# Issuing the next load ahead of the exchange of the slot that has landed

## The chip, the core and the metric

The kernel runs on one core of a Trainium2 chip. The core has a matrix engine (TensorE, PE in the profile; its weight loads are shown as PEld), a vector engine (VectorE, DVE), a scalar engine (ScalarE, ACT), a general engine (GpSimd, POOL) and an engine that here only waits and issues transfers (SyncE, SP). Sixteen DMA engines move data between the device's memory and the on-chip memory; ScalarE and SyncE each have a queue of transfers of their own, which both feed the same sixteen. The metric is the device time of one execution in microseconds; less is better.

## What is computed

```python
def reference(x, itok_B_0_7, L0_cond_weights):      # x: (128, 128, 1024) float32
    w = weights[subjects]                            # (8, 128, 128) -> (128, 128, 128)
    out = jnp.einsum('bct,bcd->bdt', x, w)
    return x + out
```

Each of 128 samples, a matrix of 128 channels by 1024 times, is multiplied by one of eight 128 x 128 weight matrices, which its index picks, and added to itself. The sum with x is had by adding the identity to the weights. Read are 64 MiB of x and 0.5 MiB of weights, written are 64 MiB.

## The kernel before

The 128 samples are handled four at a time: 32 turns (NT), each with a slot of 2 MiB of x_all, of which there are 12 (SLOTS). A slot is loaded, exchanged, multiplied, overwritten with the result and stored from the same place. A slot has two halves h (H = 2) of two samples each (G = 2).

**Load.** `load` (line 142) issues two transfers of 1 MiB on ScalarE's queue, one for each half. A transfer puts two successive channel rows of a sample on one partition, so that it moves long pieces. The two samples of a half then lie one on the lower and one on the upper 64 partitions, each with its even channels in the first 1024 columns and its odd ones in the second.

**Exchange.** `trade` (line 154) mends that on ScalarE, by six copies of 64 partitions x 1024 (line 152): for each half the upper partitions' first columns go to `spare` (tensor aside), then the lower partitions' second columns go to their place, then `spare` goes to the lower partitions' second columns. After that one sample fills all partitions, its even channels on the lower ones and its odd ones on the upper ones; weights and identity are sorted the same way at the start. The semaphore s_moved counts the copies done. At the end of the exchange s_ready is raised by two, one for each half.

**Multiply and copy.** `multiply` (line 202) waits for the weights of a half (s_go) and for s_ready, and multiplies into PSUM; `copy` (line 217, VectorE) writes the result of a half back over the slot and raises s_added; `place` (line 195, VectorE) adds weights and identity for what comes next.

**Store.** SyncE waits for s_added and issues the stores in order (lines 300 to 308): one slot each for the first 20 turns, two slots each for the last 12. The very last is issued at line 329. The first store is written from pieces of 4 KB, the others from pieces of 16 or 32 KB. GpSimd waits for each store to land and raises s_empty for the slot that became free (lines 296 to 298). s_empty starts with 7 free slots.

**What sets the order on ScalarE.** Four slots are loaded at once (AHEAD = 4, line 267). Then the loop at line 272 runs 28 times over: wait until slot i has landed (s_in), exchange it, wait for a free slot (s_empty), issue the load of slot i + 4. The last four slots are exchanged behind the loop (line 277). Each engine works through its own instructions strictly in this order, so what stands behind a wait waits too.

Of the kernel before, what the change touches and what calls it, by code (L numbers as in the profile page):

```python
# [30 lines left out]
G = 2  # L31
H = 2
# [3 lines left out]
SLOTS = 12  # L36
# [14 lines left out]
R = 2  # L51

AHEAD = 4
# [5 lines left out]
def transfer(nc, engine, out, in_):  # L59

    later, nc._always_lower_symbolic_ap = nc._always_lower_symbolic_ap, False
    ins, outs = engine.lower_ap_dma(in_), engine.lower_ap_dma(out)
    nc._always_lower_symbolic_ap = later
    return engine.add_instruction(
        mybir.InstDMACopy(
            name=nc.get_next_instruction_name(),
            engine=engine.engine,
            ins=ins,  # L70
            outs=outs,
            mode="Copy",
            cce_op=ALU.bypass,
            queue=QUEUES[engine.engine],
        )
    )
# [3 lines left out]
def kernel(  # L80
# [7 lines left out]
    nc = tc.nc  # L88
    B, C, T = x.shape
# [3 lines left out]
    def sbuf(name, *shape, dtype=F32):  # L93
        return ctx.enter_context(nc.sbuf_tensor(name, list(shape), dtype)).ap()
# [5 lines left out]
    x_all = sbuf("x_all", C, SLOTS * H * G * T)  # L100
# [6 lines left out]
    A = C // R  # L107
    eye = sbuf("eye", C, 1, D)
    mark = sbuf("mark", 1, 1)
    aside = sbuf("aside", C, T)  # L110
    spare = [aside[h * A : (h + 1) * A] for h in range(H)]
# [17 lines left out]
    s_ready = tc.alloc_semaphore("s_ready")  # L129
# [4 lines left out]
    s_eye = tc.alloc_semaphore("s_eye")  # L134
    s_moved = tc.alloc_semaphore("s_moved")
# [3 lines left out]
    def emptied(i):  # L139
        return DMA * (i // SLOTS)  # L140

    def load(k, slot, first):
        for h in range(H):
            transfer(
                nc,
                nc.scalar,
                x_all[:, bass.ds(slot * (H * G * T) + h * G * T, G * T)],
                x[bass.ds(first + h * G, G)].rearrange("h (b r) t -> (h b) (r t)", r=ROWS),
            ).then_inc(s_in[k], DMA)

    def move(out, in_):
        return nc.scalar.copy(out, in_)  # L152

    def trade(k, slot):
        nc.scalar.wait_ge(s_in[k], DMA * H).then_inc(s_in[k], -DMA * H)  # L155
        sides = [
            (
                x_all[A:, bass.ds(slot * (H * G * T) + h * G * T, T)],
                x_all[:A, bass.ds(slot * (H * G * T) + (h * G * T + T), T)],
            )  # L160
            for h in range(H)
        ]
        for h in range(H):
            move(spare[h], sides[h][0]).then_inc(s_moved, 1)
        for h in range(H):
            nc.scalar.wait_ge(s_moved, 1).then_inc(s_moved, -1)
            move(sides[h][0], sides[h][1]).then_inc(s_moved, 1)
        for h in range(H):
            nc.scalar.wait_ge(s_moved, 1).then_inc(s_moved, -1)
            move(sides[h][1], spare[h]).then_inc(s_moved, 1)  # L170
        nc.scalar.wait_ge(s_moved, H).then_inc(s_moved, -H)
        nc.scalar.wait_ge(s_eye, R).then_inc(s_ready, H)

    def store(i, n):
        at = i % SLOTS * H * G * T
# [25 lines left out]

    def multiply(slot, h):
        nc.tensor.wait_ge(s_go, 1).then_inc(s_go, -1)
        nc.tensor.wait_ge(s_ready, 1).then_inc(s_ready, -1)  # L204
        for q in range(h * G, (h + 1) * G):
            for t in range(0, T, N):
                at = slot * (H * G * T) + (q * T + t)
                mm = nc.tensor.matmul(  # L208
                    ps[h][:, q % G, t : t + N],
                    ws[q][:, 0, :],  # L210
                    x_all[:, bass.ds(at, N)],
                    start=True,
                    stop=True,
                )
        mm.then_inc(s_product, 1)
# [6 lines left out]
    with tc.tile_critical():  # L222

        nc.sync.dma_start(
            w_raw, weights.rearrange("s (u j) d -> (s u) (j d)", j=S)
        ).then_inc(s_wall, DMA)
        nc.sync.dma_start(given, subjects.rearrange("(o b) -> o b", o=1)).then_inc(s_given, DMA)

        nc.vector.memset(zeros, 0.0).then_inc(s_zeros, 1)  # L229
        nc.tensor.wait_ge(s_zeros, 1)  # L230
        for _ in range(IDLE):
            nc.tensor.matmul(  # L232
                ps[P_SLOTS - 1][:, G - 1, :N], zeros[:, :D], zeros, start=True, stop=True
            )

        nc.vector.wait_ge(s_wall, DMA)
        for r in range(R):  # L240
            nc.vector.transpose(  # L241
                w_mid.rearrange("p (e r h w j) -> p r j h e w", e=4, r=R, h=4, w=8)[:, r],
                w_raw.rearrange("p (j r d) -> p r j d", r=R, d=D)[:, r],
            ).then_inc(s_sort, 1)
        nc.vector.memset(index[:, B:], 0).then_inc(s_index, 1)
        nc.vector.wait_ge(s_given, DMA)
        nc.vector.tensor_scalar(near, given, -S, S - 1, ALU.max, ALU.min).then_inc(s_index, 1)  # L247
        nc.vector.wait_ge(s_index, 2)
        nc.vector.tensor_scalar(wrap, near, 0, S, ALU.is_lt, ALU.mult).then_inc(s_index, 1)  # L249
        nc.vector.wait_ge(s_index, 3)  # L250
        nc.vector.tensor_tensor(index[:, :B], near, wrap, ALU.add).then_inc(s_index, 1)  # L251

        nc.gpsimd.wait_ge(s_zeros, 1)
        for r in range(R):
            if r:
                nc.gpsimd.wait_ge(s_eye, r)
            nc.gpsimd.affine_select(  # L257
                eye[:, 0],
                eye[:, 0] if r else zeros[:, :D],
                [[-1, D]],  # L260
                ALU.not_equal,
                1.0,
                base=r - r * R * A,
                channel_multiplier=R,
            ).then_inc(s_eye, 1)

        for i in range(AHEAD):
            load(i % AHEAD, i, i * (H * G))
        nc.scalar.wait_ge(s_eye, R)
        nc.scalar.copy(mark, eye[:1, 0, :1])  # L270
        nc.gpsimd.wait_ge(s_eye, R).then_inc(s_empty, SLOTS - 1 - AHEAD)
        with nc.scalar.Fori(0, NT // AHEAD - 1) as turn:
            for k in range(AHEAD):
                trade(k, (turn * AHEAD + k) % SLOTS)
                nc.scalar.wait_ge(s_empty, 1).then_inc(s_empty, -1)
                load(k, (turn * AHEAD + (k + AHEAD)) % SLOTS, turn * (AHEAD * H * G) + (k + AHEAD) * H * G)
        for i in range(NT - AHEAD, NT):
            trade(i % AHEAD, i % SLOTS)

        nc.vector.wait_ge(s_sort, R)  # L280
        nc.vector.transpose(w_late, w_mid).then_inc(s_sort, 1)  # L281

        def sort(engine, o, v):
            engine.tensor_copy(  # L284
                w_all[32 * v : 32 * (v + 1), 2 * o : 2 * (o + 1), :],
                w_late[32 * o : 32 * (o + 1)].rearrange(
                    "c (e u r d) -> c u r e d", e=2, u=2, r=R
                )[:, v % 2, v // 2],
            ).then_inc(s_sort, 1)

        nc.vector.wait_ge(s_sort, R + 1)
        nc.gpsimd.wait_ge(s_sort, R + 1)
        for o in range(4):
            for v in range(4):
                sort(nc.gpsimd if v == 3 else nc.vector, o, v)
        nc.gpsimd.wait_ge(s_added, 1).then_inc(s_empty, 1)
        for i in range(SLOTS, NT):
            nc.gpsimd.wait_ge(s_slot[i % SLOTS], emptied(i)).then_inc(s_empty, 1)

        for i in [*range(NT - SLOTS), *range(NT - SLOTS, NT, PAIR)]:  # L300
            n = 1 if i < NT - SLOTS else PAIR
            nc.sync.wait_ge(s_added, (i + n) * H)
            if i == 0:
                nc.sync.dma_start(
                    out[: H * G].rearrange("g d t -> d g t"), xs[0]
                ).then_inc(s_slot[0], DMA)
            elif i + n < NT:
                store(i, n).then_inc(s_slot[i % SLOTS], DMA)


        nc.vector.wait_ge(s_index, 4)
        nc.vector.wait_ge(s_sort, SORTED)
        nc.vector.wait_ge(s_eye, R)
        subject = subjects_of(slice(0, H * G))
        for h in range(H):
            place(h, subject)
        with nc.vector.Fori(0, NT) as turn:  # L317
            subject = subjects_of(turn + 1)
            for h in range(H):
                copy(turn % SLOTS, h)  # L320
                place(h, subject)
        with nc.tensor.Fori(0, NT) as turn:
            for h in range(H):
                multiply(turn % SLOTS, h)
# [39 lines left out]
```

## Time and profile before

| | |
|---|---|
| time, median of 3 runs | 324.16 us (324.02 to 324.26) |
| the profiled execution's own time | 324.05 us |
| its span, first to last instruction | 322.1 us |
| PE busy | 247.5 us (77%) |
| ACT busy | 198.7 us (62%) |
| DVE busy | 181.5 us (56%) |
| PEld busy | 102.2 us (32%) |
| moved by the DMA engines | 134.76 MB, mean 418 GB/s |

Busy times of engines are read as shares of the span; the issue of a transfer isn't counted as busy. For the DMA engines, the share is the mean over all sixteen. A row of the timeline gives the start, the duration, the engine, the line and the operation, with the idle time ahead of it and what ended it in brackets. Rows of ACTq and SPq are issues of transfers on ScalarE's and SyncE's queues.

### The profile page before, as it was taken

How to read it: one execution, taken by the hardware profiler on the slowest of the kernel's cores; microseconds unless marked ns; L12 is line 12 of the kernel's file. 1: busy time of each engine (PE TensorE's matmuls, PEld its weight loads, DVE VectorE, ACT ScalarE, POOL GpSimd, SP SyncE). 2: the span in 40 equal slices, each digit the busy share in tenths (PEclk: the TensorE clock that was granted, in tenths of full speed). 3: DMA queues.
4: the chain of work that ended last, by engine and by line, in shares of the span. 5: the costliest groups of instructions: out<-in, count | busy, mean ns of one | idle time of the engine just before them, and what ended most of it. 6: DMA issues, size and time to landing. Idle time of an engine off the chain costs nothing. (4 is left out here: it accounts for less than half of the span.)

```text
span 322.1 us, 3002 instructions
## 1 busy us (share of the span) xinstructions
PE 247.5 (77%) x528; PEld 102.2 (32%) x528; DVE 181.5 (56%) x217; ACT 198.7 (62%) x194; POOL 2.5 (1%) x10
## 2 busy tenths in 40 slices
PE   7499988888888888888888599598884989992000
PEld 3144333333333333333333144233332434440000
DVE  4717766666666666666666617447552666775000
ACT  1777777777777777777775772757727699900000
POOL 0200000000000000000000000000000000000000
PEclk9879999999999999999999969789997999999555
DMA  8999999999999999999999999999999999999994
GB/s 326 395 452 392 407 433 433 403 429 429 435 427 427 448 423 439 413 419 423 427 437 433 442 407 423 431 431 433 446 415 411 427 454 407 429 439 431 419 431 203
DMA packets 7731, 134.76 MB, mean 418 GB/s; under 512 B 1457, under 2 KB 1458, under 8 KB 2098
## 3 DMA queue, kind: packets, MB, share of 16 engines
q1 hardware_dynamic: 4658, 67.64, 49.7%
q10 hardware_dynamic: 3072, 67.11, 49.0%
q14 instruction: 1, 0.01, 0.0%
HBM read 67.63 MB, written 67.11 MB: 418 GB/s over the span
## 5 line engine op out<-in xcount | busy, mean ns | idle before, releaser
L208 PE MATMUL ps<-x_all,w 128*128 x512 | 237.7, 619 | 42.7 <-PEq L204 42.3
L220 DVE COPY x_all<-ps 128x2048 f32 x64 | 146.7, 2292 | 107.5 <-DVEq L219 107.5
L208 PEld LDWEIGHTS ps<-x_all,w 128*128 128x128 f32 x512 | 98.2, 197 | 182.2 <-issue 182.0
L152 ACT COPY aside<-x_all 64x1024 f32 (+1 forms) x64 | 66.7, 1042 | 75.2 <-ACTq L155 74.4
L152 ACT COPY x_all<-aside 64x1024 f32 (+1 forms) x64 | 66.8, 1044 | 1.6
L152 ACT COPY x_all<-x_all (+1 forms) x64 | 63.7, 1040 | 0.8
L197 DVE TENSOR_TENSOR w<-w_all,eye 128x128 f32<-128x128 f32 x132 | 31.9, 283 | 0.8 <-issue 0.8
L232 PE MATMUL ps<-x_all 128*128 128x512 f32 x16 | 9.8, 782 | 1.7 <-DVE x_all L229 1.7
L232 PEld LDWEIGHTS ps<-x_all 128*128 128x128 f32 x16 | 4.0, 255 | 6.7 <-issue 5.0
L270 ACT ACT_TABLE_LOAD x1 | 1.3, 1283 | 6.2 <-issue 6.2
L284 DVE COPY w_all<-x_all 32x256 f32<-32x256 f32 x12 | 3.9, 327 | 0.4
L241 DVE STREAM_TRANSPOSE x_all<-x_all 128x512 f32<-128x512 f32 x2 | 2.0, 1076 | 2.9 <-DMA x_all<-in_L_cond_weights_dram 2.9
L284 POOL COPY w_all<-x_all 32x256 f32<-32x256 f32 x4 | 1.7, 426 | 6.6 <-DVE x_all L281 6.5
L281 DVE STREAM_TRANSPOSE x_all<-x_all 128x1024 f32<-128x1024 f32 x1 | 1.2, 1225 | 0.0
L229 DVE MEMSET x_all<- 128x512 f32 x1 | 0.5, 485 | 1.0 <-SPq L222 1.0
L247 DVE TENSOR_SCALAR x_all<-x_all 1x128 int32<-1x128 int32 x1 | 0.2, 215 | 0.6 <-DMA x_all<-in_itok_B_dram 0.6
L257 POOL TENSOR_SCALAR_AFFINE_SELECT eye<-x_all 128x128 f32<-128x128 f32 x1 | 0.3, 295 | 1.4 <-DVE x_all L229 1.4
L251 DVE CUSTOM_DVE_ANT_0 index<-x_all 1x256 uint16<-1x256 uint16 x1 | 0.3, 280 | 0.0
L257 POOL TENSOR_SCALAR_AFFINE_SELECT eye<-eye 128x128 f32<-128x128 f32 x1 | 0.3, 294 | 0.1
L249 DVE TENSOR_SCALAR x_all<-x_all 1x128 int32<-1x128 int32 x1 | 0.2, 214 | 0.0
L270 ACT COPY mark<-eye 1x1 f32<-1x1 f32 x1 | 0.2, 190 | 0.0
L351 POOL MEMSET const-bfloat16-1.0<- 128x1 bf16 x1 | 0.1, 102 | 0.0
(5 smaller groups left out, 0.4 us busy)
## 6 DMA issues: line engine op xcount, KB each, us to landing
x_all<-in_x_dram ACTq DMA_DIRECT2D x64, 1024.0 KB, 10.2
out_dram<-x_all SPq DMA_DIRECT2D x20, 2048.0 KB, 53.1
out_dram<-x_all SPq DMA_DIRECT2D x6, 4096.0 KB, 42.6
x_all<-in_L_cond_weights_dram SPq DMA_DIRECT2D x1, 512.0 KB, 3.5
x_all<-in_itok_B_dram SPq DMA_DIRECT2D x1, 0.5 KB
```

Of the source, the lines that this page charges most:

```text
L152: return nc.scalar.copy(out, in_)
L197: copy = nc.vector.tensor_tensor(ws[q], w_all[:, bass.ds(subject[q], 1), :], eye, ALU.add)
L208: mm = nc.tensor.matmul(ps[h][:, q % G, t : t + N], ws[q][:, 0, :], x_all[:, bass.ds(at, N)], start=True, stop=True,)
L220: nc.vector.tensor_copy(mine, ps[h].rearrange("d g t -> d (g t)")).then_inc(s_added, 1)
L229: nc.vector.memset(zeros, 0.0).then_inc(s_zeros, 1)
L232: nc.tensor.matmul(ps[P_SLOTS - 1][:, G - 1, :N], zeros[:, :D], zeros, start=True, stop=True)
L241: nc.vector.transpose(w_mid.rearrange("p (e r h w j) -> p r j h e w", e=4, r=R, h=4, w=8)[:, r], w_raw.rearrange("p (j r d) -> p r j d", r ...
L251: nc.vector.tensor_tensor(index[:, :B], near, wrap, ALU.add).then_inc(s_index, 1)
L257: nc.gpsimd.affine_select(eye[:, 0], eye[:, 0] if r else zeros[:, :D], [[-1, D]], ALU.not_equal, 1.0, base=r - r * R * A, channel_multipli ...
L270: nc.scalar.copy(mark, eye[:1, 0, :1])
L281: nc.vector.transpose(w_late, w_mid).then_inc(s_sort, 1)
L284: engine.tensor_copy(w_all[32 * v : 32 * (v + 1), 2 * o : 2 * (o + 1), :], w_late[32 * o : 32 * (o + 1)].rearrange("c (e u r d) -> c u r e ...
```

## The change

The function `trade` is split. `landed(k)` waits for slot i; the wait for a free slot and the load of slot i + 4 come next, and the exchange stands behind them. In the exchange, the two copies of the middle step become one over both halves (64 x 2 x 1024), behind a wait for both copies into `spare`; the two copies back wait for it. s_ready is raised by one for a slot, and TensorE waits for it only at the first half. The exchange doesn't wait for s_eye any more. The copy into `mark` raises s_moved by two, so that the first wait at the head of the loop is met.

```diff
-    def trade(k, slot):
+    def landed(k):
         nc.scalar.wait_ge(s_in[k], DMA * H).then_inc(s_in[k], -DMA * H)
-        sides = [
-            (
-                x_all[A:, bass.ds(slot * (H * G * T) + h * G * T, T)],
-                x_all[:A, bass.ds(slot * (H * G * T) + (h * G * T + T), T)],
-            )
-            for h in range(H)
-        ]
+
+    def trade(slot):
+        base = slot * (H * G * T)
+        both = x_all[:, bass.ds(base, H * G * T)].rearrange("c (h s t) -> c s h t", h=H, s=G)
         for h in range(H):
-            move(spare[h], sides[h][0]).then_inc(s_moved, 1)
-        for h in range(H):
-            nc.scalar.wait_ge(s_moved, 1).then_inc(s_moved, -1)
-            move(sides[h][0], sides[h][1]).then_inc(s_moved, 1)
+            move(spare[h], both[A:, 0, h]).then_inc(s_moved, 1)
+        nc.scalar.wait_ge(s_moved, 2 * H).then_inc(s_moved, -2 * H)
+        move(both[A:, 0], both[:A, 1]).then_inc(s_moved, 1)
+        nc.scalar.wait_ge(s_moved, 1).then_inc(s_moved, -1)
         for h in range(H):
-            nc.scalar.wait_ge(s_moved, 1).then_inc(s_moved, -1)
-            move(sides[h][1], spare[h]).then_inc(s_moved, 1)
-        nc.scalar.wait_ge(s_moved, H).then_inc(s_moved, -H)
-        nc.scalar.wait_ge(s_eye, R).then_inc(s_ready, H)
+            move(both[:A, 1, h], spare[h]).then_inc(s_moved, 1)
+        nc.scalar.wait_ge(s_moved, H).then_inc(s_ready, 1)
...
         nc.tensor.wait_ge(s_go, 1).then_inc(s_go, -1)
-        nc.tensor.wait_ge(s_ready, 1).then_inc(s_ready, -1)
+        if h == 0:
+            nc.tensor.wait_ge(s_ready, 1).then_inc(s_ready, -1)
...
-        nc.scalar.copy(mark, eye[:1, 0, :1])
+        nc.scalar.copy(mark, eye[:1, 0, :1]).then_inc(s_moved, H)
...
             for k in range(AHEAD):
-                trade(k, (turn * AHEAD + k) % SLOTS)
+                landed(k)
                 nc.scalar.wait_ge(s_empty, 1).then_inc(s_empty, -1)
-                load(k, (turn * AHEAD + (k + AHEAD)) % SLOTS, turn * (AHEAD * H * G) + (k + AHEAD) * H * G)
+                load(
+                    k,
+                    (turn * AHEAD + (k + AHEAD)) % SLOTS,
+                    turn * (AHEAD * H * G) + (k + AHEAD) * H * G,
+                )
+                trade((turn * AHEAD + k) % SLOTS)
         for i in range(NT - AHEAD, NT):
-            trade(i % AHEAD, i % SLOTS)
+            landed(i % AHEAD)
+            trade(i % SLOTS)
```

On ScalarE, one turn of the loop (that of slot 0 and of the load of slot 4) stands in this order before; ISA rows set registers or wait, and the names in brackets are the semaphores waited for:

```order
L152 ISA [waits s_in0]
L152 COPY aside<-x_all 64x1024
L152 ISA
L152 COPY aside<-x_all 64x1024
L152 ISA [waits s_moved]
L152 COPY x_all<-x_all 64x1024
L152 ISA [waits s_moved]
L152 COPY x_all<-x_all 64x1024
L152 COPY x_all<-aside 64x1024 [waits s_moved] x2
L64 ISA [waits s_moved,s_eye,s_empty]
L64 ISA
L66 DMA x_all<-in_x_dram 128x2048
```

The same turn of the changed kernel, from its wait for slot 0 to the last copy back:

```order
L64 ISA [waits s_in0,s_empty]
L64 ISA
L66 DMA x_all<-in_x_dram 128x2048
L64 ISA
L66 DMA x_all<-in_x_dram 128x2048
L152 ISA
L152 COPY aside<-x_all 64x1024
L152 ISA
L152 COPY aside<-x_all 64x1024
L152 ISA [waits s_moved]
L152 COPY x_all<-x_all 64x2x1024
L152 COPY x_all<-aside 64x1024 [waits s_moved]
```

The load and the wait for a free slot have moved from behind the copies to ahead of them, and one double copy stands where two single ones stood.

At the end of ScalarE's loop, before, the wait for the last free slot and the last load close the loop, and the exchange of slot 28 follows:

```order
L152 COPY x_all<-aside 64x1024 [waits s_moved] x2
L64 ISA [waits s_moved,s_eye,s_empty]
L64 ISA
L66 DMA x_all<-in_x_dram 128x2048
L64 ISA
L66 DMA x_all<-in_x_dram 128x2048
L272 REGISTER_ALU
L272 COMPARE_AND_BRANCH
L152 COPY aside<-x_all 64x1024 [waits s_in0]
```

In the changed kernel the exchange of slot 27 stands between the last load and the loop's end:

```order
L66 DMA x_all<-in_x_dram 128x2048
L152 ISA
L152 COPY aside<-x_all 64x1024
L152 ISA
L152 COPY aside<-x_all 64x1024
L152 ISA [waits s_moved]
L152 COPY x_all<-x_all 64x2x1024
L152 COPY x_all<-aside 64x1024 [waits s_moved]
L152 ISA
L152 COPY x_all<-aside 64x1024
L268 REGISTER_ALU [waits s_moved]
L268 COMPARE_AND_BRANCH
```

Five exchanges now stand behind the last load where four stood. The transfers, their sizes and their number are the same.

## The prediction

> **What bounds the kernel now.** First the transfers over the whole span, since the kernel reads and writes 64 MiB each and computes little per byte. The page's slices (each a fortieth of the span, the tenths being the busy share of the 16 DMA engines) and its queue rows (packets, MB, share of the 16 engines' time):
>
> ```profile
> DMA  8999999999999999999999999999999999999994
> DMA packets 7731, 134.76 MB, mean 418 GB/s; under 512 B 1457, under 2 KB 1458, under 8 KB 2098
> q1 hardware_dynamic: 4658, 67.64, 49.7%
> q10 hardware_dynamic: 3072, 67.11, 49.0%
> ```
>
> Every slice but the first and the last is at 9, and the stores (q1) and loads (q10) together took 98.7% of what 16 engines had to give in 322.1 us. Next the same by stage, in the view of windows (window, its length, busy time of PE, PEld, DVE, ACT, POOL, then TensorE's granted clock, the DMA share and GB/s):
>
> ```profile
> 0.00:4.00 4.00, 2.33 (x3) 1.18 (x4) 0.51 (x2) 0.00 (x0) 0.79 (x6) 1.00 0.57 172
> 4.00:28.00 24.00, 18.91 (x35) 7.59 (x34) 13.43 (x27) 15.34 (x16) 1.71 (x4) 0.86 1.00 430
> 28.00:44.00 16.00, 14.58 (x34) 6.10 (x33) 11.42 (x15) 11.47 (x12) 0.00 (x0) 1.00 1.00 394
> 44.00:172.00 128.00, 110.27 (x249) 45.88 (x248) 82.66 (x91) 96.11 (x95) 0.00 (x0) 1.00 1.00 429
> 172.00:256.00 84.00, 66.86 (x134) 27.30 (x133) 44.84 (x52) 51.10 (x50) 0.00 (x0) 0.90 1.01 430
> 256.00:268.00 12.00, 10.81 (x26) 4.51 (x25) 7.89 (x10) 11.04 (x11) 0.00 (x0) 1.00 0.98 418
> 268.00:292.00 24.00, 23.73 (x54) 9.62 (x52) 18.06 (x21) 13.61 (x14) 0.00 (x0) 1.00 1.02 432
> 292.00:316.00 24.00, 0.00 (x0) 0.00 (x0) 2.69 (x3) 0.00 (x0) 0.00 (x0) 0.61 1.00 429
> 316.00:322.00 6.00, 0.00 (x0) 0.00 (x0) 0.00 (x0) 0.00 (x0) 0.00 (x0) 0.50 0.31 131
> ```
>
> From 4 to 316 us the DMA share is 1.00, and the rate stays near 430 GB/s whether loads run alone (4 to 28), both directions (44 to 256) or stores alone (292 to 316). Only 28 to 44 is poorer, at 394. Last, what waits at the end: the chain's last piece, SyncE's last issue and its last wait.
>
> ```profile
> 294.34 0.48 DVE w L197 x2
> 295.12 0.56 SPq L66 DMA_DIRECT2D out_dram<-x_all  x1
> SPq L360 <- DMA out_dram<-x_all: 25.4, 1, 25.4
> ```
>
> All computing is over at 294.8, and then 25.4 us go to stores that were queued. So **the DMA engines bound the whole kernel**. A load that starts earlier only goes ahead of a store on the same engines. The sum: 0.57 x 4 + 24 + 16 + 128 + 84.8 + 11.8 + 24.5 + 24 + 0.31 x 6 = 317 us of work for 16 engines, and some 5 us of start and end that the change doesn't touch. No byte, no packet size and no store is changed.
>
> **The change part by part.** One slot's turn on ScalarE, from the timeline (start, duration, in brackets the idle time ahead), and the costs of single copies:
>
> ```profile
> 58.28 1.15 ACTq L66 DMA_DIRECT2D x_all<-in_x_dram  x2
> 59.79 2.11 ACT L152 COPY aside<-x_all 64x1024 f32 x2 [2.01 <-ACTq L155]
> 61.92 1.99 ACT L152 COPY x_all<-x_all  x2
> 63.94 2.11 ACT L152 COPY x_all<-aside 64x1024 f32 x2
> 66.55 1.15 ACTq L66 DMA_DIRECT2D x_all<-in_x_dram  x2
> 7.48 0.19 ACT L270 COPY mark<-eye 1x1 f32<-1x1 f32 x1
> 263.05 2.11 ACT L152 COPY aside<-x_all 64x1024 f32<-64x1024 f32 x2 [0.30 <-ACTq L155]
> L152 ACT COPY x_all<-x_all (+1 forms) x64 | 63.7, 1040 | 0.8
> ```
>
> A turn takes 66.55 - 58.28 = 8.27 us: 1.15 for the two DMA issues, 0.36 to the first copy, 6.26 of exchange (59.79 to 66.05) and 0.50 to the next issue. ScalarE never waits for data here: it is itself the pace of the loads, one 2.1 MB slot in 8.27 us, 254 GB/s of the 429, and the stores get the rest.
>
> *The middle copies become one.* A copy of one element took 0.19 us and one of 1024 per partition 1.04, so 0.85 is per 1024 elements; 0.19 + 2 x 0.85 = 1.89 us in place of 1.99. That saves 0.10.
>
> *Fewer waits, but each for the copy just ahead.* Before, the copies go in two independent strands (h = 0 and 1), so that a copy waits for the one two places back, and the gaps between pairs are 0.02 us. After, the double copy waits for both copies ahead, and the copies back wait for the double copy. The nearest row of such a wait is the 0.30 us ahead of the exchange at 263.05, where the next exchange waits for the last copy of the one before. Two of these: +0.60, less the two gaps of 0.02. The exchange becomes 2.11 + 0.30 + 1.89 + 0.30 + 2.11 = 6.71 us, **0.45 longer, not shorter**. Bounds: 6.11 with no bubble at all (0.15 shorter); 7.30 if the double copy costs two whole ones (2.08) and each bubble is like the 0.50 ahead of an issue (1.04 longer). I take 6.71, as the 0.30 row is the same kind of wait. A turn then takes 8.72 us and loads flow at 240 GB/s; stores take what is left. In the sum for the end it is nothing while the store queue has work, and it does: stores land 53 us after their issue.
>
> ```profile
> out_dram<-x_all SPq DMA_DIRECT2D x20, 2048.0 KB, 53.1
> ```
>
> The wait on s_eye that goes had been met before the copy into mark at 7.48, which waits for it too, and TensorE's second wait on s_ready was met by the same signal as its first. Both are at nothing; a gain is excluded because neither was ever the last thing waited for.
>
> *The load ahead of the exchange.* The first two issues move from 16.53 to about 10, when slot 0 has landed; the first exchange starts some 1.5 us later and ends 2 later, and so does the first store.
>
> ```profile
> 9.76 2.11 ACT L152 COPY aside<-x_all 64x1024 f32 x2 [2.09 <-ACTq L155]
> 16.53 1.16 ACTq L66 DMA_DIRECT2D x_all<-in_x_dram  x2
> ```
>
> The load queue wasn't dry at 16.53 (DMA share 1.00 from 4 to 28), so this fills no hole: **0 us**. Its bounds are what the poor stretch from 28 to 44 can give or take, 1.3 us either way (B and C below).
>
> *The wait for a free slot now stands ahead of the exchange.* From 172 us on the loads are held by s_empty. What is queued behind that wait on ScalarE is now the exchange of a slot that has long landed, and behind it TensorE, VectorE and SyncE. While eight older slots are waiting to be stored, nobody on the DMA side sees it. At the end it counts. The rows there (ScalarE; TensorE with 16 matmuls a slot; VectorE's last copy):
>
> ```profile
> 255.06 1.16 ACTq L66 DMA_DIRECT2D x_all<-in_x_dram  x2
> 256.48 2.11 ACT L152 COPY aside<-x_all 64x1024 f32<-64x1024 f32 x2 [2.79 <-ACTq L155]
> 263.21 28.68 PE L208 MATMUL ps<-x_all,w 128*128 x64 [1.19 <-PEq L204]
> 206.09 17.17 PE L208 MATMUL ps<-x_all,w 128*128 x32 [3.39 <-PEq L204]
> 224.84 7.13 PE L208 MATMUL ps<-x_all,w 128*128 x16 [1.58 <-PEq L204]
> ```
>
> The last load goes out at 255.06 when store 19 has landed, which the DMA rate sets and the change leaves. Before, slot 27 was exchanged by then and four remained. After, five remain: 27 starts at 256.48 and is ready at 263.2, TensorE starts it at 263.7 and needs 28.68 / 4 = 7.17 us a slot for five, more than ScalarE's 6.71 + 0.30, so till 299.6; VectorE ends 2.9 later (294.8 against 263.21 + 28.68 = 291.9), and the last store is issued at 302.8 in place of 295.1. The DMA engines come to it when? It and what follows is two slots, 4.19 MB, 9.8 us at 429. Stores end at about 316 + 0.31 x 6 = 317.9, so its turn is at 308.1. With about 1 us from issue to first packet (the first packets begin by 4 - 0.57 x 4 = 1.7 us, the first issue stands at 0.91), **4 us of slack are left of 12**. If the wait lets TensorE's clock fall, 17.17 - 2 x 7.13 = 2.9 us more go, and 1 is left.
>
> By the Trainium skill, "TensorE: Matmul & The Clock Gate", Part 1, about 3.4 us of idleness bring the clock to half. The trace agrees (17.17 us after a gap of 3.39, none of it after 1.58). By that rule the wait moved ahead of the exchange costs TensorE its clock, as reckoned above; without it the last store would be in time by 4 us rather than 1.
>
> **Sum**: 0 at the start, 0 in the middle, 0 at the end, under the cover of the store queue. The profiled execution took 324.05 us, against a median of 324.16: the changed kernel takes 324.1.
>
> **The rivals.**
> *A: the tail is uncovered (slower).* If the exchange costs its upper bound, ScalarE rather than TensorE paces the five last slots: 256.48 + 5 x (7.30 + 0.30) = 294.5, then 0.5 + 7.2 + 2.9 make 305.1, with 2.9 for the clock 308.0, and the last store is issued at 308.3 and has packets at 309.3, 1.2 us late. A free-slot signal later by another us adds as much; together 326.3. It decides once the last store is issued after 307. For it: the margin is the smallest in the kernel, and both steps that eat it are this change's. Against: it needs both upper bounds.
> *B: the dip at 28 to 44 us heals (faster).* It is worth (430 - 394) x 16 us / 430 = 1.3 us, hence 322.7. There store 0, written from 4 KB pieces (the page counts 2098 - 1458 = 640 packets between 2 and 8 KB), meets the loads. The changed kernel has a longer load queue there and store 0 comes 2 us later, so the mixture is another. For: it is the only poor stretch. Against: the same pieces and the same loads are still to be moved.
> *C: the dip gets deeper,* since more loads are queued when store 0's small pieces come: doubled, +1.3 us, 325.4.
> *D: the DMA rate as such rises.* In the trace the best long stretch, 432, lies 0.6% above the 429 of the middle, so at most 128 + 84 us x 0.006 = 1.3 us, again 322.8; nothing in the change alters packets, so I count it with B.
> The Trainium skill's "DMA: Bandwidth & Descriptors", Where 436 GB/s comes from, gives 435 GB/s as the ceiling of the 16 engines; by it an estimate of the least transfer time is 134.76 MB / 435 = 310 us, 7 below the 317 used, but no stretch here holds it.
> That the change doesn't do what it says, as the loads after 172 us are held by free slots and not by the exchange, gives the forecast's time as well.
>
> **How the numbers follow.** A measurement of this kernel tells about 0.2% (0.65 us) from no change. Forecast 0.72 (within 0.2%), A 0.10, C 0.08, B and D 0.10. So faster 0.10, same 0.72, slower 0.18. The range takes in the forecast, most of B (322.9) and C and nearly all of A (326.0); about 0.1 is left out.
>
> **What would show it.** Right: DMA share 1.00 from 4 to 316 us again; the first pair of loads issued near 10 us; an exchange of about 6.7 us with two gaps of 0.3; turns of 8.7 us up to about 170 us; last store issued near 303 to 306, and SyncE's last wait down from 25.4 to some 15 us. Wrong: a window after 292 us with a DMA share under 0.95 (A), or a rate between 28 and 44 us that isn't 394 (B, C). What would overturn the whole: a time below 322, as it would need bytes moved faster than in any stretch of this trace.

## The result, and the profile after

| | time, median | range | ratio to the kernel before |
|---|---|---|---|
| before, beside it | 324.11 us (13 runs) | 323.88 to 324.34 | |
| changed | 323.59 us (13 runs) | 323.14 to 323.92 | 0.9983 (0.9975 to 0.9992) |

The kernel is 0.17% faster, 0.5 us, which lies within the 0.2% of the forecast and in its range. The profiled execution took 323.66 us, with a span of 321.7.

The DMA queues of the changed kernel (packets, MB, share of 16 engines) and its slices:

```profile
DMA  8999999999999999999999999999999999999994
q1 hardware_dynamic: 4658, 67.64, 49.7%
q10 hardware_dynamic: 3072, 67.11, 48.9%
```

The same packets, and 98.6% of what 16 engines had. The windows of the changed kernel (TensorE's clock, DMA share and GB/s are the last three columns):

```profile
4.00:28.00 24.00, 17.43 (x32) 6.99 (x31) 12.11 (x27) 13.62 (x13) 1.71 (x4) 0.86 1.00 427
28.00:44.00 16.00, 14.26 (x33) 5.91 (x32) 11.81 (x13) 12.13 (x10) 0.00 (x0) 1.00 1.06 437
44.00:172.00 128.00, 107.48 (x239) 44.50 (x237) 79.77 (x91) 87.76 (x73) 0.00 (x0) 0.99 1.00 426
172.00:256.00 84.00, 64.09 (x130) 26.32 (x131) 44.95 (x51) 51.82 (x43) 0.00 (x0) 0.92 1.00 428
268.00:292.00 24.00, 23.80 (x55) 9.81 (x53) 18.44 (x21) 20.13 (x17) 0.00 (x0) 1.00 1.01 430
292.00:316.00 24.00, 7.45 (x17) 2.95 (x16) 8.07 (x9) 0.00 (x0) 0.00 (x0) 0.77 1.01 429
```

The DMA share stays at 1.00 up to 316 us. What moved is inside: TensorE and VectorE now work into the window from 292 on (7.45 and 8.07 us, where before there were 0 and 2.69). The poor stretch from 28 to 44 has gone from 394 to 437 GB/s; but the window behind it, first of the kernel before and then of the changed one, shows where it went:

```profile
44.00:60.00 16.00, 13.46 (x31) 5.54 (x30) 10.67 (x12) 11.85 (x13) 0.00 (x0) 1.00 1.02 435
```

```profile
44.00:60.00 16.00, 13.35 (x31) 5.43 (x29) 9.25 (x13) 11.62 (x10) 0.00 (x0) 1.00 0.95 400
```

From 28 to 60 us together that is (394 + 435) / 2 = 414.5 before and 418.5 after: 4 GB/s over 32 us, 0.3 us of transfer time. A piece counts in the window in which it begins, so a share can exceed 1.00 (1.06 beside the 437), and single windows swing by some per cent.

ScalarE's first turn in the timeline of the changed kernel, and the tail: ScalarE's last load with the exchange of slot 27 behind it, TensorE's last five slots, SyncE's last two issues (a merged row, from the first's start to the second's end) and its last wait:

```profile
10.22 1.16 ACTq L66 DMA_DIRECT2D x_all<-in_x_dram  x2
11.55 2.11 ACT L152 COPY aside<-x_all 64x1024 f32 x2 [3.86 <-issue]
13.85 1.90 ACT L152 COPY x_all<-x_all  x1 [0.19 <-ACTq L162]
15.86 2.11 ACT L152 COPY x_all<-aside 64x1024 f32 x2
18.45 1.15 ACTq L66 DMA_DIRECT2D x_all<-in_x_dram  x2
```

```profile
255.44 1.16 ACTq L66 DMA_DIRECT2D x_all<-in_x_dram  x2
256.77 2.11 ACT L152 COPY aside<-x_all 64x1024 f32 x2 [1.83 <-issue]
```

```profile
263.61 35.90 PE L204 MATMUL ps<-x_all,w 128*128 x80 [1.12 <-PEq L200]
```

```profile
287.70 15.59 SPq L66 DMA_DIRECT2D out_dram<-x_all  x2
```

```profile
SPq L362 <- DMA out_dram<-x_all: 17.4, 1, 17.4
```

The first loads go out at 10.22 in place of 16.53. At the end TensorE does five slots in one go behind the last load, till 299.5, and the last store's issue ends at 303.3, 7.6 us later than before (295.12 + 0.56 = 295.7); SyncE waits 17.4 us for it in place of 25.4. Those 7.6 us came out of the cover, the time in which stores that are already queued keep the DMA engines busy, and not out of the time of the kernel.

### The profile page after: what moved, and what is told of

The parts are those of the page before. It is cut to its first block, busy times and chain, and to the rows that moved or that the text cites. A ratio compares the mean times of both kernels' runs of the same rounds, so it can differ in the third digit from the quotient of the medians.

```text
span 321.7 us, 2843 instructions
## 1 busy us (share of the span) xinstructions
PE 247.7 (77%) x528; PEld 102.2 (32%) x528; DVE 181.4 (56%) x217; ACT 195.7 (61%) x162; POOL 2.5 (1%) x10
## 5 line engine op out<-in xcount | busy, mean ns | idle before, releaser
L152 ACT COPY x_all<-x_all (+1 forms) x32 | 60.7, 1897 | 6.2 <-ACTq L162 5.7
```

## The experiments

The kernels that end in "again" are the same as their namesakes, run side by side on another chip.

| run | time | ratio to the kernel before (interval) |
|---|---|---|
| e1, before, store 0 from 16 KB | 323.90 us | 0.9991 (0.9980 to 1.0002) |
| e2, changed, store 0 from 16 KB | 323.63 us | 0.9983 (0.9974 to 0.9991) |
| e3, reorder alone | 324.20 us | 1.0000 (0.9991 to 1.0009) |
| e11, reorder alone, again | 324.24 us | 0.9997 (0.9988 to 1.0006) |
| e4, double copy alone | 324.01 us | 0.9991 (0.9980 to 1.0002) |
| e12, double copy alone, again | 323.65 us | 0.9974 (0.9964 to 0.9984) |
| e10, the changed kernel again | 323.98 us | 0.9992 (0.9982 to 1.0002) |
| e7, no exchange | 323.23 us | 0.9960 (0.9945 to 0.9975) |
| e5, 4 more copies at the end | 323.97 us | 0.9991 (0.9981 to 1.0000) |
| e6, 8 more copies at the end | 326.82 us | 1.0086 (1.0046 to 1.0126) |
| e8, 2.1 MB fewer stored | 320.18 us | 0.9858 (0.9829 to 0.9887) |
| e9, last store split | 333.13 us | 1.0249 (1.0222 to 1.0275) |

The kernel before was at 324.37 us beside e1 to e4, at 324.27 beside e5 to e8 and at 324.37 beside e9 to e12.

### Is the exchange covered? (e7)

The changed kernel without its five copies a slot:

```diff
     def trade(slot):
-        base = slot * (H * G * T)
-        both = x_all[:, bass.ds(base, H * G * T)].rearrange("c (h s t) -> c s h t", h=H, s=G)
-        for h in range(H):
-            move(spare[h], both[A:, 0, h]).then_inc(s_moved, 1)
-        nc.scalar.wait_ge(s_moved, 2 * H).then_inc(s_moved, -2 * H)
-        move(both[A:, 0], both[:A, 1]).then_inc(s_moved, 1)
-        nc.scalar.wait_ge(s_moved, 1).then_inc(s_moved, -1)
-        for h in range(H):
-            move(both[:A, 1, h], spare[h]).then_inc(s_moved, 1)
         nc.scalar.wait_ge(s_moved, H).then_inc(s_ready, 1)
```

> The changed kernel without any copy of the exchange (left out: the exchange, so samples are mixed up in the output). Theory (the DMA engines bound the whole kernel and ScalarE's copies are covered to the last one): 323 to 324 us, as the changed kernel, with 196 us of ScalarE's work gone. Rival (the turn of ScalarE paces the loads for 140 us, and that costs something at the end): several us faster.

323.23 us, as the theory had it: with nearly all of ScalarE's 196 us of work gone, the kernel gains 1.0 us on the kernel before, 0.36 to 0.75 on the two medians of the changed one, which were not taken beside it. So a faster exchange could have been worth 1.0 us at most. Two rows of its windows show why, the one after the start and the one at the end:

```profile
28.00:44.00 16.00, 15.84 (x37) 6.53 (x36) 11.22 (x14) 0.00 (x0) 0.00 (x0) 1.00 1.03 435
292.00:316.00 24.00, 4.56 (x11) 1.71 (x9) 5.69 (x8) 0.00 (x0) 0.00 (x0) 0.68 1.00 426
```

ScalarE is at 0.00, and the transfers run at the rate that they had with it. Even the 1.0 us may not be the exchange's. The last windows of e7:

```profile
317.00:318.00 1.00, 0.00 (x0) 0.00 (x0) 0.00 (x0) 0.00 (x0) 0.00 (x0) 0.50 0.77 328
318.00:319.00 1.00, 0.00 (x0) 0.00 (x0) 0.00 (x0) 0.00 (x0) 0.00 (x0) 0.50 0.16 66
319.00:320.00 1.00, 0.00 (x0) 0.00 (x0) 0.00 (x0) 0.00 (x0) 0.00 (x0) 0.50 0.00 0
```

The kernel before has shares of 0.77, 0.08 and 0.08 there. A share of 0.08 is one piece of one engine, some 1.3 us (0.08 x 16). So e7 has one piece more before 319 us and none after it: its last piece comes about 1 us earlier, and its profiled execution took 322.91 us, 1.1 less than that of the kernel before. Whether that comes of leaving out the exchange was not tested.

### Do the bytes set the end? (e8)

```diff
-                store(i, n).then_inc(s_slot[i % SLOTS], DMA)
+                store(i, 1 if i == NT - 2 * PAIR else n).then_inc(s_slot[i % SLOTS], DMA)
```

> The changed kernel with the store of slots 28 and 29 cut to slot 28 (left out: the write of slot 29, 2.1 MB). Theory (bytes over 429 GB/s set the end): 4.9 us faster, 318.7, as the last store's data are ready 4.8 us ahead of its turn. Rival (the end hangs on the last slot's computing): less than 2 us faster.

The runs took 318.95 to 322.31 us, with a median of 320.18; against 323.59 to 323.98 of the changed kernel that is 3.4 to 3.8 less, and the fastest run comes within 0.3 of the expected 318.7. The other three (319.65, 320.71 and 322.31) fall short of it, and the slowest is the profiled one. TensorE's tail and the windows there:

```profile
265.73 38.94 PE L204 MATMUL ps<-x_all,w 128*128 x80 [4.88 <-PEq L200]
```

```profile
302.00:304.00 2.00, 2.00 (x6) 0.88 (x5) 2.00 (x3) 0.00 (x0) 0.00 (x0) 1.00 0.64 270
304.00:306.00 2.00, 0.67 (x2) 0.00 (x0) 1.33 (x3) 0.00 (x0) 0.00 (x0) 1.00 0.06 25
306.00:308.00 2.00, 0.00 (x0) 0.00 (x0) 1.60 (x3) 0.00 (x0) 0.00 (x0) 1.00 0.00 0
308.00:310.00 2.00, 0.00 (x0) 0.00 (x0) 0.00 (x0) 0.00 (x0) 0.00 (x0) 0.85 0.61 262
```

Here TensorE stood for 4.88 us ahead of slot 27 and needed 38.94 us for the five slots in place of 35.90; these 3 us are a lost clock (0.91 granted from 256 to 292 us, 1.00 in the changed kernel's first profile). VectorE works till nearly 308, while the DMA engines, which by then have a slot less to do, stand empty from 304 to 308. So the bytes set the end as long as the last data are ready; with one slot less they no longer always are.

### How thick is the cover at the end? (e5, e6)

Four or eight copies more ahead of the exchange of slot 31, each waited for:

```diff
             landed(i % AHEAD)
+            if i == NT - 1:
+                nc.scalar.wait_ge(s_moved, H).then_inc(s_moved, -H)
+                for _ in range(4):
+                    move(spare[0], x_all[A:, i % SLOTS * H * G * T :][:, :T]).then_inc(s_moved, 1)
+                    nc.scalar.wait_ge(s_moved, 1).then_inc(s_moved, -1)
+                nc.scalar.copy(mark, eye[:1, 0, :1]).then_inc(s_moved, H)
             trade(i % SLOTS)
```

> The changed kernel with 4 more copies (1.04 us each and a wait of 0.1 to 0.3 behind each) ahead of the exchange of slot 31: about 5 us, of which TensorE, which is 2.7 us behind ScalarE there, sees 2.3 to 3. The last store then goes out at about 306 in place of 303.3. Theory (it is covered until 307): time of the changed kernel within 0.3 us, about 323.6. Rival (the tail is uncovered, or some of the end hangs on the last store): slower by 2 to 3 us.

> The same with 8 more copies, about 10 us: the exchange of slot 31 ends near 299.6, TensorE starts it after a gap of 7 us at half clock and ends near 310, and the last store goes out near 313. Theory (cover ends at 307): uncovered by 5 to 6 us, about 329. A rival that would hold the store queue for deeper than reckoned: no change, 323.6. A rival without a loss of clock: 326.

e5 took 323.97 us, 0.9991 of the kernel before; the changed kernel had 0.9983 and 0.9992: no loss that can be told. SyncE's last two issues and the windows from 304 to 310 in e5, then the same in e6:

```profile
287.42 19.93 SPq L66 DMA_DIRECT2D out_dram<-x_all  x2
```

```profile
304.00:306.00 2.00, 0.00 (x0) 0.00 (x0) 2.00 (x1) 0.00 (x0) 0.00 (x0) 1.00 0.96 410
306.00:308.00 2.00, 0.00 (x0) 0.00 (x0) 0.50 (x3) 0.00 (x0) 0.00 (x0) 1.00 0.88 377
308.00:310.00 2.00, 0.00 (x0) 0.00 (x0) 0.00 (x0) 0.00 (x0) 0.00 (x0) 0.65 1.12 475
```

```profile
289.45 22.63 SPq L66 DMA_DIRECT2D out_dram<-x_all  x2
```

```profile
306.00:308.00 2.00, 2.00 (x6) 0.74 (x4) 1.86 (x3) 0.00 (x0) 0.00 (x0) 1.00 0.73 311
308.00:310.00 2.00, 0.29 (x1) 0.00 (x0) 1.47 (x1) 0.00 (x0) 0.00 (x0) 1.00 0.04 16
310.00:312.00 2.00, 0.00 (x0) 0.00 (x0) 1.22 (x3) 0.00 (x0) 0.00 (x0) 1.00 0.00 0
312.00:314.00 2.00, 0.00 (x0) 0.00 (x0) 0.00 (x0) 0.00 (x0) 0.00 (x0) 0.72 0.92 393
```

In e5 the last issue ends at 307.35. The share of 0.88 is no hole: 1.12 follows, and the changed kernel has 0.85 in the same window with its last issue ended at 303.3. In e6 the last issue ends at 312.1, and the engines stand empty from about 307.5 (0.73 of the window from 306 to 308) to 312. **The cover ends close to where it was reckoned, at 307.**

The price of e6, 2.6 us over the kernel before and 2.8 to 3.2 over the two medians of the changed one, is about half of the 5 to 6 expected. About 1 us of the miss is in the issue, at 312 and not 313. For the rest the runs suggest that the end before was not the end of all engines, which the last section takes up: the four windows add up to 4.6 us of empty engines, but the profiled execution, 325.95 us, is only 2.0 to 2.3 above the two profiled ones of the changed kernel. The time is near that of the rival without a loss of clock, 326, but the clock was lost: the last slot took TensorE 8.56 us in place of 7.13.

The changed kernel came to the edge of its cover by itself. In its second profile (e10) the last load went out at 257.25 in place of 255.44, and TensorE's tail and SyncE's last two issues were these:

```profile
265.54 38.59 PE L204 MATMUL ps<-x_all,w 128*128 x80 [4.88 <-PEq L200]
```

```profile
292.31 15.60 SPq L66 DMA_DIRECT2D out_dram<-x_all  x2
```

The clock was lost as in e8, the last issue ended at 307.9, and of the slack nothing was left. The execution took 323.98 us, and no window of it after 292 us stands empty (0.88 from 306 to 308, 1.12 behind it).

### Where do the 0.5 us come from? (e1 to e4, e10 to e12)

First idea: store 0's small pieces meet the loads from 28 to 44 us. Store 0 issued like the other stores:

```diff
-            if i == 0:
-                nc.sync.dma_start(
-                    out[: H * G].rearrange("g d t -> d g t"), xs[0]
-                ).then_inc(s_slot[0], DMA)
-            elif i + n < NT:
+            if i + n < NT:
```

> The kernel before, with store 0 issued like the other stores (pieces of 16 KB in place of 4 KB). Theory (the poor stretch from 28 to 44 us, 394 GB/s, is store 0's small pieces meeting the loads): that stretch comes to about 430 GB/s and the time falls by 1.3 us or a little more, to 322.5 to 323. Rival (the stretch is poor because the load queue runs dry or for another reason than the pieces): the stretch stays near 394 GB/s and the time within 0.3 us of the kernel before.

> The changed kernel with the same edit of store 0. Theory: the change saved about 0.5 us by letting store 0 meet the loads in another way, so that with 16 KB pieces nothing of this is left to save: the time is that of the kernel before with the same edit, within 0.3 us, at 322.5 to 323. Rival (the change saves its 0.5 us elsewhere): this one stays 0.5 us under the kernel before with the same edit.

**The theory fell.** In e1 the stretch comes to 407 GB/s and not to 430, and the time, 323.90 us in place of the expected 322.5 to 323, moves by 0.0009 with an interval that holds 1:

```profile
28.00:44.00 16.00, 14.84 (x35) 6.21 (x34) 11.86 (x15) 11.34 (x12) 0.00 (x0) 1.00 1.01 407
44.00:60.00 16.00, 13.45 (x32) 5.58 (x31) 10.47 (x11) 11.84 (x13) 0.00 (x0) 1.00 1.00 424
```

e2 has the ratio of the changed kernel, 0.9983, which speaks against the pieces of store 0 as what the 0.5 us hang on. It lies 0.27 us under e1, between its two expectations, so by itself it doesn't decide.

Second, each half of the change alone. The reorder alone takes the loop of the change (wait for the slot, free slot, load, exchange) with the six copies of before. The double copy alone keeps the loop of before (cut from the edit):

```diff
         for h in range(H):
-            move(spare[h], sides[h][0]).then_inc(s_moved, 1)
-        for h in range(H):
-            nc.scalar.wait_ge(s_moved, 1).then_inc(s_moved, -1)
-            move(sides[h][0], sides[h][1]).then_inc(s_moved, 1)
+            move(spare[h], both[A:, 0, h]).then_inc(s_moved, 1)
+        nc.scalar.wait_ge(s_moved, H).then_inc(s_moved, -H)
+        move(both[A:, 0], both[:A, 1]).then_inc(s_moved, 1)
+        nc.scalar.wait_ge(s_moved, 1).then_inc(s_moved, -1)
         for h in range(H):
...
+            move(both[:A, 1, h], spare[h]).then_inc(s_moved, 1)
```

> The kernel before with the load put ahead of the exchange alone; six copies and all waits as before. Theory (what changes at 28 to 44 us is that the load queue is longer when store 0 comes): the rate there rises towards 430 GB/s and the time is that of the changed kernel, about 0.5 us under the kernel before. Rival (the copies and waits did it): the time of the kernel before, within 0.2 us.

> The kernel before with the double copy and its waits alone; the load stays behind the exchange. Theory (ScalarE is covered by the store queue): the time of the kernel before within 0.2 us, the exchange about 6.4 us in place of 6.25, and 28 to 44 us still near 394 GB/s. Rival: 0.5 us faster, as the changed kernel.

> The changed kernel once more, beside its two halves on the same chip. Theory (its 0.5 us are real and come of the whole): 0.998 of the kernel before. Rival (they lie within what the chips and runs give): within 0.1% of its halves and of the kernel before.

> The load put ahead of the exchange alone, once more (1.0000 before, 0.9991 to 1.0009). Theory (the halves are worth nothing that can be told apart): within 0.1% of the kernel before and of the changed kernel. Rival (the reorder carries the gain): 0.998.

> The double copy alone, once more (0.9991 before, 0.9980 to 1.0002). Theory: within 0.1% of the kernel before and of the changed kernel. Rival (the double copy carries the gain): 0.998.

The reorder alone gives 1.0000 and 0.9997: nothing, twice, as the rival had it in e3 and the theory in e11, although it moves the poor stretch from 28-44 to 44-60 as the changed kernel does (e11):

```profile
28.00:44.00 16.00, 14.40 (x34) 5.94 (x33) 11.90 (x13) 12.16 (x12) 0.00 (x0) 1.00 1.07 437
44.00:60.00 16.00, 13.03 (x31) 5.27 (x29) 9.60 (x13) 12.32 (x12) 0.00 (x0) 1.00 0.94 395
```

The double copy alone gives 0.9991 and 0.9974, and leaves the stretch where it was (e12):

```profile
28.00:44.00 16.00, 14.71 (x34) 6.10 (x33) 12.29 (x15) 10.89 (x9) 0.00 (x0) 1.00 0.98 392
44.00:60.00 16.00, 13.07 (x31) 5.44 (x30) 9.72 (x10) 12.14 (x10) 0.00 (x0) 1.00 1.04 441
```

So the poor stretch is not the source. What there is of a gain seems to go with the double copy: the changed kernel and the double copy alone lie 0.1 to 0.3% under the kernel before, which is the rival's case in e12 and between the two expectations in e4. It isn't shown. The second run of the changed kernel (e10, 0.9992, the rival's case) and the first of the double copy (0.9991) have intervals that hold 1; e1, which has six copies, is at 0.9991 as well; and side by side, the whole change (e10) gains less than its half (e12). The profiled executions of the double copy took 324.09 and 324.30 us, no less than that of the kernel before (324.05), so no trace here holds the gain. What the double copy could save the transfers is open. But for e1 the runs order themselves by how much ScalarE does (six copies, five, none: 324.1 to 324.4, 323.6 to 324.0, 323.2 us), but copies, waits and recorded instructions (3002, 2843 to 2906, 2507) fall together in them, and no run took them apart.

### The engine that ends last (e9)

The function `store` takes a range of partitions (LAST is 120); cut from the edit:

```diff
...
             elif i + n < NT:
                 store(i, n).then_inc(s_slot[i % SLOTS], DMA)
+            else:
+                store(i, n, LAST, C).then_inc(s_slot[i % SLOTS], DMA)
...
-    last = store(NT - PAIR, PAIR)
+        nc.scalar.wait_ge(s_slot[(NT - PAIR) % SLOTS], emptied(NT - PAIR + SLOTS))
+    last = store(NT - PAIR, PAIR, 0, LAST)
```

> The changed kernel with the last store split: partitions 120 to 127 first, then 0 to 119. In the traces one DMA engine writes alone for about 2 us at the end (DMA share 0.08 of 16). Theory (that engine is the one that serves the highest partitions, and is late by itself): it is spared one last share and the time falls by 0.5 to 1.5 us against the changed kernel, to 322 to 323. Rival (it is another engine): 0 to 1.2 us slower, as the others get one more piece of 1.23 us.

333.13 us, 9 slower, far outside both theories. The windows of e9's end:

```profile
304.00:308.00 4.00, 0.06 (x1) 0.00 (x0) 2.69 (x3) 0.00 (x0) 0.00 (x0) 1.00 0.96 410
308.00:320.00 12.00, 0.00 (x0) 0.00 (x0) 0.00 (x0) 0.00 (x0) 0.00 (x0) 0.50 0.94 205
```

The engines are nearly as busy as ever (0.94) and move half as much (205 GB/s): the last store, split into 8 and 120 partitions, goes at about half the rate of the whole one. Why was not found, and no run took the two parts apart. It says nothing on which engine is late.

## Why the prediction was right

- **What bounds the kernel.** Right: the DMA share is 1.00 to 316 us in the changed kernel, the exchange taken away altogether gains 1.0 us at most, and a slot's bytes taken away 3.4 to 3.8, up to 5 in the fastest run.
- **The load ahead of the exchange fills no hole, 0 us.** Right: first loads at 10.22 us, and the reorder alone is at 1.0000 and 0.9997.
- **The exchange.** The mechanism was right, the size was not. The double copy takes 1.90 us (1.89 reckoned). The two bubbles are 0.19 (ahead of 13.85) and 0.11 (from 15.75 to 15.86) and not 0.30 each, so the exchange takes 17.97 - 11.55 = 6.42 us, 0.16 longer than before where 0.45 was reckoned. The 0.30 had been read between two exchanges. The first copy also follows the issue 0.17 us later and not 0.36, so that the first turn takes 18.45 - 10.22 = 8.23 us. Over the even turns the mean is 8.40 us (15 turns from 10.22 to 136.27) against 8.31 before (18 turns from 16.53 to 166.14) and 8.72 reckoned: the loads flow nearly as they did. The even turns end at 136 us, where the first long one (10.62 us) stands, and not at about 170 as foretold. None of this reached the time.
- **The tail.** Right to half a microsecond at each step on the way to the last store: exchange of slot 27 at 256.77 (256.48 reckoned), TensorE at 263.61 (263.7) for 35.90 us (35.9), the last store's issue ended at 303.3 (begun at 302.8 by the reckoning). SyncE's last wait was 17.4 (some 15). That holds for the first profile and is luck in part: in e10's, of the same kernel, the last load went out 1.8 us later, TensorE lost its clock, and the last issue ended 4.6 us later, at 307.9. The 4 us of slack were those of one execution; the 1 us reckoned for a lost clock left out the later load. And the length of the gap alone doesn't tell whether the clock is lost: 2.69 us ahead of the last slot in e5 cost it (8.82 us for 16 matmuls), 3.28 us ahead of the slot at 255.36 in the changed kernel did not (7.13).
- **Rival A, the uncovered tail.** Its point of decision, 307 us, was tested from both sides: e5 with an issue ended at 307.35 and e10 with 307.9 lose nothing that can be told, e6 with 312.1 loses about 3 us.
- **Rivals B, C and D, the rate.** B's picture came true (394 to 437 GB/s) and its price didn't: the dip moved on by 16 us, and the reorder that moves it is worth nothing. A rate other than 394 had been named as a sign that the prediction is wrong; it came, and it was none. D's higher rate did not come (426 from 44 to 172 us, 429 before); its 432 lies 0.7% and not 0.6% above 429, which makes 1.5 us and changes no chance. The cause that was named, store 0's 4 KB pieces, explains about a third of the dip at most: with 16 KB pieces the stretch has 407 and not 430.
- **The sum.** 324.1 was given, 323.59 measured. The difference, 0.5 us, lies within the 0.2% that the prediction allowed for. What may stand behind it is a term taken as 0: a gain of 0.1 to 0.3% with the double copy, which is not shown and whose cause stays open.

## What to carry to other kernels

Where the DMA share is 1.00 from end to end and the same bytes are to be moved, issuing a load earlier only changes who waits in the queue; look at what the reorder puts behind the wait instead, and reckon the time from the last load to the last store against what is left in the store queue then. That cover can be measured by adding work in steps at that place, and it should be read from more than one execution: here the last store was issued at 303.3 in one and at 307.9 in another. A stretch with a poor rate that "heals" must be looked for in the window behind it before it is counted.

## What the runs showed of the hardware

The end of these kernels is not the end of all 16 DMA engines. The last windows of the changed kernel:

```profile
317.00:318.00 1.00, 0.00 (x0) 0.00 (x0) 0.00 (x0) 0.00 (x0) 0.00 (x0) 0.50 0.16 66
318.00:319.00 1.00, 0.00 (x0) 0.00 (x0) 0.00 (x0) 0.00 (x0) 0.00 (x0) 0.50 0.00 0
319.00:320.00 1.00, 0.00 (x0) 0.00 (x0) 0.00 (x0) 0.00 (x0) 0.00 (x0) 0.50 0.08 33
```

Packets are counted where they begin: 33 GB/s in 1 us is one piece of 32 KB, begun after 319 when the others had begun their last before 318. One engine writes alone for 1 to 2 us, and it did so in the kernel before as well as in the reorder and double copy runs; not in e7, e6 and e8. In e6, where all engines ran empty ahead of the last store, they also ended together (shares of 1.22 and 1.23 from 320 to 322 us, 0.01 behind). The lateness was taken up by the gap and didn't come back, which is likely one reason why e6 cost less than reckoned. Which engine it is and why it is late was not found. And the last store split into 8 and 120 partitions moved 205 GB/s at a share of 0.94 (e9), where the whole one goes at 429.
